# Moving two pre-pass steps across a pair boundary, and sharing a subtraction between GpSimd and VectorE, in a four-layer attention kernel

## The chip, the cores and the metric

The kernel runs on one core of a Trainium2 chip. The metric is the device time of one execution in microseconds (us). The kernel before took 4373.35 us in the median of three runs (4364.13 to 4380.87); less is better.

A core has engines that each work through their own queue in order: TensorE for matrix products (PE in the profile, with its weight loads as PEld), VectorE (DVE), ScalarE (ACT), GpSimd (POOL), and SyncE (SP), whose queue here issues most of the transfers. They wait for one another through semaphores. Matrix products are written to PSUM, from where VectorE and ScalarE read them; everything else lies in SBUF.

## The reference

The input is `x` of shape (4, 32, 32, 384) in float32, four images of 1024 positions with 384 channels. Four layers follow, each with a normalisation before and a residual sum after it. Two of them matter here.

Layer 0 is attention with six heads of 64 channels. The keys and values come from positions that are sampled with learned offsets, and a bias is sampled bilinearly from a table:

```python
attn = jnp.einsum('bmhc,bnhc->bhmn', qh, k) * scale
...
attn = jax.nn.softmax(attn + bias, axis=-1)
out = jnp.einsum('bhmn,bnhc->bmhc', attn, v).reshape(Bq, Hq, Wq, NC)
```

Layer 1 is attention with twelve heads of 32 channels. Its softmax is multiplied by a weight that comes from a second, coarse similarity, and is then divided by column sums:

```python
sim = jax.nn.sigmoid(sim_beta + sim_alpha * jnp.einsum('bhnd,bhmd->bhnm', _l2norm(xg_h), _l2norm(gc)))
group_weight = jnp.einsum('bhnm,bhkm->bhnk', sim, sim)
gamma = jax.nn.sigmoid(group_gamma)
group_weight = group_weight * gamma + (1.0 - gamma)
attn = jax.nn.softmax(jnp.einsum('bhnd,bhmd->bhnm', q, k) * scale, axis=-1)
attn = attn * group_weight
attn = attn / (attn.sum(axis=2, keepdims=True) + 1e-08)
out = jnp.einsum('bhnm,bhmd->bhnd', attn, v)
```

Layer 2 takes ratios of box sums, layer 3 is a local attention over 3 x 3 neighbourhoods. The change doesn't touch them.

## The kernel before

**Two lanes.** The work of an image is split into a front lane (layer 0) and a trunk lane (layers 1 to 3). Layer 0 of image 0 runs first by itself, in another form (`heads0`). From then on `Net.layer3` steps through the trunk of image b and, by the weights that the generators yield, lets the front lane of image b+1 run in between. So while images 0, 1 and 2 are in their trunk, the heads of the next image's layer 0 are mixed into the same queues; image 3's trunk has nothing beside it. Within the order in which the program names the instructions, a scheduler places them on the engines by priority, by the buffers that come free, and by `issue_after`, which holds a block of instructions behind a named one.

**The front lane's heads** (`Front.head0`). A head is done in two halves of 512 queries; 12 halves an image, 36 in all for images 1 to 3. For each of eight blocks of 128 keys (`j`), GpSimd gathers a window of the bias table (L944), ScalarE and VectorE interpolate it in two directions (L956, L957, L961, L962), two matmuls (L968) give the scores, and VectorE adds them to the bias (L971) and keeps a running maximum `rmax` (L973, L975). After the eighth block the maximum over keys is wanted for every query, in every partition: `rmax` is transposed on PE (L982), VectorE takes the maximum `top` (L986), GpSimd multiplies it by the identity matrix (L988, `diag`, 128 x 512), PE multiplies that by ones (L990), and ScalarE copies the result to `tb` (L994). Then, for each block, VectorE subtracts `tb` from the scores (L1001), ScalarE takes exponentials (L1002), and PE multiplies them with the values (L1003).

**The trunk lane's pairs** (`Trunk.pair`). Layer 1 takes its twelve heads in six pairs, p = 0 to 5. The keys are in eight blocks of 128, j = 0 to 7. For each block and each half of the queries, PE computes scores for the two heads (L1699) into one of the two tiles called `big`, and ScalarE takes their exponential (L1707). The logarithm of the softmax's denominators has been put into an extra row of the queries, so that these exponentials are the softmax already. GpSimd scales the similarity block `sg` (L1682). Then `product(h, r)` runs four times: PE forms the group weights by transposing what an earlier block has kept (L1724) and by multiplying `sg` with `sim` (L1729), VectorE multiplies them onto the softmax with a running sum (L1736), and ScalarE keeps what later blocks need (L1741). `values` scales the values by the column sums (L1662, L1663, L1665) and multiplies (L1671), one block behind.

**The pre-pass.** The denominators of pair p+1 are computed while pair p runs. That takes eight steps, `sums_step(i)`, one for each block of 128 queries. A step takes both `big` tiles: four matmuls (L1561), then for each tile a maximum on VectorE (L1570) and an exponential with a sum on ScalarE (L1574), both at high priority. Only after that is the tile free for the next scores. The results collect in `nmax` and `den` (one buffer each). In the kernel before the eight steps of pair p are placed so: two at j = 0, two at j = 1, one each at j = 2 to 5, either between the second and third product or after the fourth. At the end of j = 5, `sums_log` turns the sums into logarithms (L1592 to L1598), and `load_sums(p + 2)` reloads the pre-pass's own copies `q4` and `k4` by four SP transfers (L1522, L1523). At j = 6, `sums_row` transposes the result (L1605, L1607) and `load_lse` puts it into the next pair's queries. Also at j = 6, after that, `sims(0)`, and at j = 7 `sims(1)`, compute the next pair's coarse similarity: four matmuls each into both `big` tiles (L1618), a tanh on ScalarE (L1627) and an addition on VectorE (L1630).

The last pair (p = 5) has no pre-pass. Pair 0's successor is prepared in pair 0 itself, and the first pair's own before the loop.

Of the kernel before, what the change touches and what calls it, by code (L numbers as in the profile page):

```python
# [21 lines left out]
ALU = mybir.AluOpType  # L22
# [4 lines left out]
P = 128  # L27
# [5 lines left out]
NH1, HD1 = 12, 32  # L33
# [33 lines left out]
def bc(ap, axis, n):  # L67

    u = ap.unsqueeze(axis)
    shape = list(u.shape)  # L70
    shape[axis] = n
    return u.broadcast_to(shape)
# [357 lines left out]
class Front(Lane):  # L430
# [500 lines left out]
    def head0(self, h, q):  # L931

        nc, v = self.nc, self.nc.vector
        f = self.f
        k, r0 = h // 2, (h % 2) * GC
        rows = slice(r0, r0 + GC)
        HH, HN = HW // 2, N // 2
        queries = self.qpad[rows, k, 1 + HH * q : 1 + HH * (q + 1), 1 : 1 + HW]
        logits = []
        rmax = self.wt([P, HN], "rmax", 2)  # L940
        for j in range(NJ):
            c = j * G + h
            win = self.wt([P, (HH + 1) * WROW], "win", 4)
            nc.gpsimd.indirect_dma_start(  # L944
                out=win,
                out_offset=None,
                in_=self.strips[:, :],
                in_offset=bass.IndirectOffsetOnAxis(
                    ap=self.widx[:, q, c : c + 1], axis=0
                ),  # L950
            )
            wv = win.rearrange("p (r c) -> p r c", c=WROW)
            sc = lambda i, t: f[:, i, t, c : c + 1]

            z = self.wt([P, HH, HW + 1], "z", 3)
            nc.scalar.activation(z, wv[:, 0:HH, 0 : HW + 1], AF.Copy, scale=sc(1, 1))  # L956
            v.scalar_tensor_tensor(  # L957
                z, wv[:, 1 : HH + 1, 0 : HW + 1], sc(0, 1), z, ALU.mult, ALU.add
            )
            lg = self.wt([P, HH, HW], "lg", 13)  # L960
            nc.scalar.activation(lg, z[:, :, 0:HW], AF.Copy, scale=sc(1, 0))  # L961
            v.scalar_tensor_tensor(lg, z[:, :, 1 : HW + 1], sc(0, 0), lg, ALU.mult, ALU.add)  # L962
            logits.append(lg.rearrange("p y x -> p (y x)"))
            if j % 2:
                ps = [self.bank() for _ in range(2)]
                for u in range(2):
                    w, mov = self.logits_of(h, q, j - 1 + u)
                    nc.tensor.matmul(ps[u], w, mov, start=True, stop=True)  # L968
                for u in range(2):
                    lf = logits[j - 1 + u]  # L970
                    v.tensor_tensor(lf, ps[u], lf, ALU.add)  # L971
                    if j - 1 + u == 1:
                        v.tensor_tensor(rmax, logits[0], lf, ALU.max)  # L973
                    elif j > 1:
                        v.tensor_tensor(rmax, rmax, lf, ALU.max)  # L975
                yield 6


        NI = HN // P
        ps = self.bank()  # L980
        for i in range(NI):
            nc.tensor.transpose(  # L982
                ps[:, i * P : (i + 1) * P], rmax[:, i * P : (i + 1) * P], self.ident
            )
        top = self.wt([P, NI], "top", 2)
        v.tensor_reduce(top, ps.rearrange("p (i n) -> p i n", i=NI), AX.X, ALU.max)  # L986
        diag = self.wt([P, NI, P], "diag", 1)
        nc.gpsimd.tensor_tensor(diag, bc(self.ident, 1, NI), bc(top, 2, P), ALU.mult)  # L988
        ps = self.bank()
        nc.tensor.matmul(  # L990
            ps, self.ones, diag.rearrange("p i n -> p (i n)"), start=True, stop=True
        )
        tb = self.wt([P, HN], "tb", 2)
        nc.scalar.copy(tb, ps)  # L994
        yield 3


        po = self.bank()
        for j in range(NJ):
            lf = logits[j]  # L1000
            v.tensor_tensor(lf, lf, tb, ALU.subtract)  # L1001
            nc.scalar.activation(lf, lf, AF.Exp)  # L1002
            nc.tensor.matmul(po, self.values_of(h, j), lf, start=j == 0, stop=j == NJ - 1)  # L1003
            if j % 2:
                yield 2

        nc.scalar.copy(queries, po[rows, :].rearrange("p (y x) -> p y x", y=HH))
        den = self.sums_of(h, po, logits[0])
        nc.sync.dma_start(self.den[h][:, q * HN : (q + 1) * HN], den)
        yield 3  # L1010
# [303 lines left out]
class Trunk(Lane):  # L1314
# [317 lines left out]
    def pair(self, p):  # L1632
# [1 line left out]


        nc, v = self.nc, self.nc.vector
        st = self.sums_state() if p + 1 < NH1 // 2 else None
        qa, ka = self.qks[p % 2]
        sim = self.sim
        if p == 5:  # L1640
# [38 lines left out]
        for j in range(NJ):  # L1679
# [66 lines left out]
            for h, r in parts[:split]:  # L1746
                last = product(h, r)
            with self.tc.issue_after(last):
                if st and j < 2:
                    self.sums_step(2 * j, st)  # L1750
                elif st and j < 6:
                    self.sums_step(j + 2, st)
                elif st and j == 6:
                    self.sums_row(p + 1, logs)
                    self.load_lse(p + 1)
                    self.sims(0)
            yield 7
            for h, r in parts[split:]:
                last = product(h, r)
            with self.tc.issue_after(last):  # L1760
                if st and j < 2:
                    self.sums_step(2 * j + 1, st)
                elif st and j == 7:
                    self.sims(1)
            if late:
# [1 line left out]
            late.append((j, es, tot))  # L1767
            if st and j == 5:
                logs = self.sums_log(st)
                if p + 2 < NH1 // 2:  # L1770
                    self.load_sums(p + 2)
            yield 7
        values(*late.pop())
        y = self.wt([P, 512], "y")
# [378 lines left out]
```

## Time and profile before

| what | value |
|---|---|
| median of three runs | 4373.35 us (4364.13 to 4380.87) |
| profiled execution | 4344.14 us, of which span 4342.2 us |
| mean granted clock of TensorE | 0.949 |
| busy: PE / VectorE / ScalarE / GpSimd | 90% / 72% / 53% / 22% of the span |
| chain that ended last: PE / VectorE / ScalarE | 49% / 27% / 9% of the span |
| a pair of layer 1, images 0 to 2 | about 119 to 126 us |
| a pair of layer 1, image 3 | about 77 us |

The profile is one execution, and it was 29 us shorter than the median. In a row of groups of instructions stand the line of the kernel, the engine, the operation, what it writes and reads by the program's names, the shape and the number of instructions; after the first bar their busy time in us and the mean duration of one in ns; after the second the idle time of that engine just before them, and what ended most of it. In a row of the timeline stand the start and the duration in us, then the same, and in brackets the idle time before. In a row of windows stand the stretch, its length, the busy time of PE, PEld, VectorE, ScalarE and GpSimd with the number of instructions, the granted clock of TensorE, the share of the DMA engines and the GB/s. Lines are those of the kernel before; in the kernel after, those behind L1001 are higher by one and, from L1753 on, by up to nine.

### The profile page before, as it was taken

What the parts mean: (1) busy time and instruction counts of PE and PEld (TensorE: products, weight loads), DVE (VectorE), ACT (ScalarE), POOL (GpSimd) and SP (SyncE); (2) the same over time, 40 slices, a digit from 0 to 9 for tenths busy, and PEclk for the clock granted to TensorE, in tenths of its full rate; (3) what the DMA queues carried; (4) which work ended last, traced back from release to release, by engine and by line L of the source; (5) the groups of instructions that cost most, each with busy time, mean ns of one, the idle gap of its engine ahead of it and who ended that gap; (6) DMA issues with size and microseconds to landing.
All of it is one profiled execution on the core that took longest, in us unless ns stands there. A gap on an engine that the chain in (4) does not pass through costs nothing.

```text
span 4342.2 us, 45288 instructions
## 1 busy us (share of the span) xinstructions
PE 3921.3 (90%) x14832; PEld 1681.8 (39%) x14832; DVE 3109.8 (72%) x5905; ACT 2304.8 (53%) x3638; POOL 963.9 (22%) x979
## 2 busy tenths in 40 slices
PE   8788989998999898999899989889889999999998
PEld 4333434333334443433333444333333434444444
DVE  4799676878887456787878746578887874566654
ACT  3366344666664334566766423366676642566633
POOL 1754152212121105221212101431121301000000
PEclk9999989998999998999999999899999999999999
DMA  7744353212221455321212154432221214311111
GB/s 161 236 122 118 89 157 106 64 42 81 60 81 40 127 140 147 108 65 46 75 54 81 40 159 143 132 103 60 61 75 47 75 41 134 99 43 26 33 34 44
DMA packets 295397, 385.08 MB, mean 89 GB/s; under 512 B 167858, under 2 KB 228798, under 8 KB 294650
## 3 DMA queue, kind: packets, MB, share of 16 engines
q1 hardware_dynamic: 246336, 217.44, 17.7%
q0 software_dynamic: 39936, 145.53, 11.3%
q10 hardware_dynamic: 8890, 19.23, 1.3%
q8 instruction: 118, 1.93, 0.2%
q14 instruction: 117, 0.96, 0.1%
HBM read 295.63 MB, written 86.75 MB: 88 GB/s over the span
## 4 chain that ended last, share of the span: by engine, by line
PE 49%; DVE 27%; ACT 9%; issue 8%; DMA 4%; POOL 3%; SPq 0%; DVEq 0%; ACTq 0%; POOLq 0%
PE bank L1729 10%; PE big L1699 6%; DVE nmax L1570 4%; PE big L407 4%; PE bank L1003 4%; DVE e L1736 3%; PE bank L421 3%; PE big L1561 3%; ACT big L1574 3%; PE bank L1724 2%; PE bank L1671 2%; PE big L667 2%; DVE z L1122 2%; PE bank L968 2%; DMA win<-strips,widx 2%
## 5 line engine op out<-in xcount | busy, mean ns | idle before, releaser
L1729 PE MATMUL bank<-whole,sg 128*128 128x512 f32 (+3 forms) x2304 | 854.4, 501 | 7.7 <-POOL sg L1682 6.2
L1736 DVE SCALAR_TENSOR_TENSOR e<-bank,gam,e 128x512 f32<-128x512 f32 x768 | 560.4, 747 | 309.9 <-PE bank L1729 189.2
L1574 ACT ACTIVATE big<-big,nmax 128x1024 f32<-128x1024 f32 x384 | 417.5, 1087 | 295.9 <-DVE nmax L1570 294.1
L1729 PEld LDWEIGHTS bank<-whole,sg 128*128 128x128 f32 x2304 | 401.7, 197 | 357.8 <-issue 272.1
L1699 PE MATMUL big<-qa,ka 64*128 64x512 f32 x1536 | 451.6, 669 | 86.7 <-ACT big L1574 82.5
L1570 DVE TENSOR_REDUCE nmax<-big 128x1 f32<-128x1024 f32 x384 | 451.9, 1217 | 62.8 <-PE big L1561 62.8
L1707 ACT ACTIVATE e<-big 128x1024 f32<-128x1024 f32 x384 | 382.1, 1020 | 176.3 <-PE big L1699 166.8
L944 POOL DMA_INDIRECT win<-strips,widx x288 | 314.8, 1093 | 699.8 <-DVE z L957 382.2
L1682 POOL TENSOR_SCALAR sg<-whole,gam 128x512 f32<-128x512 f32 x192 | 149.1, 777 | 1348.1 <-PE bank L1729 1073.0
L1561 PE MATMUL big<-k,q 32*128 32x512 f32 x1536 | 270.2, 670 | 41.6 <-ACT big L1574 30.5
L1699 PEld LDWEIGHTS big<-qa,ka 64*128 64x128 f32 x1536 | 146.9, 197 | 345.1 <-ACT big L1574 177.9
L1003 PE MATMUL bank<-lg,va 128*128 128x512 f32 x576 | 268.2, 607 | 12.9 <-ACT lg L1002 12.9
L751 POOL DMA_INDIRECT gat<-pairs,sidx x192 | 214.6, 1118 | 290.5 <-DVE ix_one L550 233.2
L962 DVE SCALAR_TENSOR_TENSOR lg<-z,bias_f,lg 128x512 f32<-128x512 f32 x288 | 216.3, 768 | 48.9 <-ACT lg L961 47.3
L956 ACT ACTIVATE z<-win,bias_f 128x528 f32<-128x528 f32 x288 | 205.3, 736 | 57.2 <-DVE lg L962 26.2
L1001 DVE TENSOR_TENSOR lg<-lg,tb 128x512 f32<-128x512 f32 x288 | 182.0, 689 | 74.7 <-ACT tb L994 74.7
L957 DVE SCALAR_TENSOR_TENSOR z<-win,bias_f,z 128x528 f32<-128x528 f32 x288 | 214.9, 763 | 20.9 <-ACT z L956 19.0
L1671 PE MATMUL bank<-e,vs 128*32 128x512 f32 x1536 | 210.7, 617 | 17.7 <-DVE vs L1665 17.7
L1741 ACT COPY gn<-bank 128x128 f32<-128x128 f32 (+2 forms) x288 | 106.3, 370 | 209.6 <-DVE e L1736 208.7
L961 ACT ACTIVATE lg<-z,bias_f 128x512 f32<-128x512 f32 x288 | 199.9, 716 | 16.8 <-DVE z L957 13.2
L971 DVE TENSOR_TENSOR lg<-bank,lg 128x512 f32<-128x512 f32 x288 | 191.3, 683 | 12.7 <-PE bank L968 12.0
L968 PE MATMUL bank<-qs,kz 64*128 64x512 f32 x288 | 172.5, 683 | 12.2 <-DVE e L1736 8.5
(326 smaller groups left out, 6315.1 us busy)
## 6 DMA issues: line engine op xcount, KB each, us to landing
q<-qd SPq DMA_DIRECT2D x48, 256.0 KB
xg<-xgd SPq DMA_DIRECT2D x48, 256.0 KB
pairs<-gat SPq DMA_DIRECT2D x48, 192.0 KB
w<-in_gmat SPq DMA_DIRECT2D x15, 576.0 KB
w<-in_Wqkv SPq DMA_DIRECT2D x12, 576.0 KB
a<-in_x SPq DMA_DIRECT2D x16, 384.0 KB
q<-qpad SPq DMA_DIRECT2D x12, 512.0 KB
qs<-q SPq DMA_DIRECT2D x24, 256.0 KB
```

Source lines behind the costliest of these rows:

```text
L944: nc.gpsimd.indirect_dma_start(out=win, out_offset=None, in_=self.strips[:, :], in_offset=bass.IndirectOffsetOnAxis(ap=self.widx[:, q, c : ...
L962: v.scalar_tensor_tensor(lg, z[:, :, 1 : HW + 1], sc(0, 0), lg, ALU.mult, ALU.add)
L968: nc.tensor.matmul(ps[u], w, mov, start=True, stop=True)
L1003: nc.tensor.matmul(po, self.values_of(h, j), lf, start=j == 0, stop=j == NJ - 1)
L1561: nc.tensor.matmul(ps[r][:, h * 512 : (h + 1) * 512], self.q4[rows, i * P : (i + 1) * P], self.k4[rows, 0:512], start=True, stop=True,)
L1570: top = v.tensor_reduce(nmax[:, r, i : i + 1], ps[r], AX.X, ALU.max, negate=True)
L1574: nc.scalar.activation(ps[r], ps[r], AF.Exp, bias=nmax[:, r, i : i + 1], accum_out=den[:, r, i : i + 1],)
L1671: nc.tensor.matmul(av[r0 : r0 + HD1, :], vs[:, r, :], es[h][:, r, :], start=j == 0, stop=j == NJ - 1,)
L1699: nc.tensor.matmul(ps[:, r, :], ka[rows, j * P : (j + 1) * P], qa[rows, cols], start=True, stop=True,)
L1707: nc.scalar.activation(e, ps, AF.Exp)
L1729: last = nc.tensor.matmul(ps[:, (mid - i0) * P :], sg[:, r, m, :], sim[:, h, r, m, (mid - i0) * P :], start=m == 0, stop=m == 1,)
L1736: v.scalar_tensor_tensor(e[:, r, :], ps, self.gam[:, 1:2], e[:, r, :], ALU.add, ALU.mult, accum_out=tot[:, r, h : h + 1],)
```

## The change

There are two edits that have nothing to do with each other.

In `Front.head0`, the diagonal is made by VectorE rather than GpSimd, and the subtraction of the maxima goes to GpSimd for every second block (j odd). Over 36 halves that takes 36 instructions from GpSimd and gives it 144, and the reverse on VectorE. `heads0`, the form for image 0, stays.

In `Trunk.pair`, steps 0 and 1 of a pre-pass move to the end of the pair before: step 0 to the middle of j = 6, after `sums_row`, and step 1 to the middle of j = 7. `sims(0)` goes from the middle of j = 6 to its end. The buffers `nmax` and `den` for it are taken at j = 6, after `sums_log` has read the old ones, and are handed on in `self.st`. `load_sums(p + 2)`, which the moved steps need, goes from the end of j = 5 to its middle, right after step 7. Pair 0 keeps two steps at j = 0 and at j = 1, since nothing ran before it. So pairs 1 to 4 have one step in each of j = 0 to 5, and pairs 0 to 3 one more at j = 6 and at j = 7. That moves 8 steps an image, 32 in all.

```diff
-        nc.gpsimd.tensor_tensor(diag, bc(self.ident, 1, NI), bc(top, 2, P), ALU.mult)
+        v.tensor_tensor(diag, bc(self.ident, 1, NI), bc(top, 2, P), ALU.mult)
...
         for j in range(NJ):
             lf = logits[j]
-            v.tensor_tensor(lf, lf, tb, ALU.subtract)
+            eng = nc.gpsimd if j % 2 else v
+            eng.tensor_tensor(lf, lf, tb, ALU.subtract)
             nc.scalar.activation(lf, lf, AF.Exp)
...
-        st = self.sums_state() if p + 1 < NH1 // 2 else None
+        st, self.st = (self.st if p else self.sums_state()), None
...
             with self.tc.issue_after(last):
-                if st and j < 2:
+                if st and p == 0 and j < 2:
                     self.sums_step(2 * j, st)
                 elif st and j < 6:
                     self.sums_step(j + 2, st)
+                    if j == 5 and p + 2 < NH1 // 2:
+                        self.load_sums(p + 2)
                 elif st and j == 6:
                     self.sums_row(p + 1, logs)
                     self.load_lse(p + 1)
-                    self.sims(0)
+                    if p + 2 < NH1 // 2:
+                        self.st = self.sums_state()
+                        self.sums_step(0, self.st)
+                    else:
+                        self.sims(0)
+                elif self.st:
+                    self.sums_step(1, self.st)
             yield 7
...
             with self.tc.issue_after(last):
-                if st and j < 2:
+                if st and p == 0 and j < 2:
                     self.sums_step(2 * j + 1, st)
+                elif st and j == 6 and self.st:
+                    self.sims(0)
                 elif st and j == 7:
                     self.sims(1)
...
             if st and j == 5:
                 logs = self.sums_log(st)
-                if p + 2 < NH1 // 2:
-                    self.load_sums(p + 2)
             yield 7
```

## The prediction

> **What bounds the kernel now.** I read the page's busy times first, then its costliest groups, then the idle time of TensorE (PE) slot by slot through all 24 pairs of heads, then windows of the places that the change touches, then single steps in the timeline.
>
> ```profile
> PE 3921.3 (90%) x14832; PEld 1681.8 (39%) x14832; DVE 3109.8 (72%) x5905; ACT 2304.8 (53%) x3638; POOL 963.9 (22%) x979
> ...
> L1574 ACT ACTIVATE big<-big,nmax 128x1024 f32<-128x1024 f32 x384 | 417.5, 1087 | 295.9 <-DVE nmax L1570 294.1
> ...
> L1699 PE MATMUL big<-qa,ka 64*128 64x512 f32 x1536 | 451.6, 669 | 86.7 <-ACT big L1574 82.5
> L1570 DVE TENSOR_REDUCE nmax<-big 128x1 f32<-128x1024 f32 x384 | 451.9, 1217 | 62.8 <-PE big L1561 62.8
> ...
> L1001 DVE TENSOR_TENSOR lg<-lg,tb 128x512 f32<-128x512 f32 x288 | 182.0, 689 | 74.7 <-ACT tb L994 74.7
> ```
>
> PE is busy 90% of the span, so only about 421 us are idle, and the largest single cause of that idle time is one edge: the scores L1699 waiting 82.5 us for L1574, the exponentials of a pre-pass step. A step fills both "big" tiles, VectorE (DVE) takes two maxima, ScalarE (ACT) two exponentials, and only then may another matmul write there. In the timeline, one step of image 3 and, last, the scores after the worst wait and after none:
>
> ```profile
> 3961.74 1.14 PE L1561 MATMUL big<-k,q 32*128 32x512 f32 x8
> 3962.98 2.36 DVE L1570 TENSOR_REDUCE nmax<-big 128x1 f32<-128x1024 f32 x2 [0.31 <-PE big L1561]
> 3964.30 1.09 ACT L1574 ACTIVATE big<-big,nmax 128x1024 f32<-128x1024 f32 x1 [1.22 <-DVE nmax L1570]
> 3965.43 1.09 ACT L1574 ACTIVATE big<-big,nmax 128x1024 f32<-128x1024 f32 x1
> 3965.55 0.30 PEld L1699 LDWEIGHTS big<-qa,ka 64*128 64x128 f32 x4 [1.04 <-ACT big L1574]
> 3966.68 0.30 PEld L1699 LDWEIGHTS big<-qa,ka 64*128 64x128 f32 x4 [0.83 <-ACT big L1574]
> ```
>
> ```profile
> 1032.11 3.78 PE L1699 MATMUL big<-qa,ka 64*128 64x512 f32 x8 [5.10 <-ACT big L1574]
> ```
>
> ```profile
> 4050.03 1.99 PE L1699 MATMUL big<-qa,ka 64*128 64x512 f32 x8
> ```
>
> From a step's first matmul the first tile is free after 3.8 us (3961.74 to 3965.55), the second after 4.95 (3966.68). And the eight score matmuls after a 5.10 us gap took 3.78 us instead of 1.99: PE restarted at half rate, worth 1.8 us more. I see the same after gaps of 3.25, 2.44, 1.91 and 1.27 us, and not after 0.9 to 1.2.
>
> The last view is the windows. The first two rows are the end of pair 2 (j=6, 7) and the start of pair 3 (j=0, 1) in image 0, the last two the same places in image 3, where no layer-0 lane runs beside.
>
> ```profile
> 975.00:1006.30 31.30, 24.13 (x103) 11.35 (x107) 29.20 (x64) 17.63 (x27) 9.01 (x9) 0.80 0.31 88
> 1006.30:1053.90 47.60, 39.25 (x126) 14.46 (x120) 43.02 (x72) 39.10 (x65) 18.93 (x18) 0.89 0.40 117
> ```
>
> ```profile
> 4044.60:4058.70 14.10, 14.10 (x97) 7.60 (x99) 10.11 (x29) 9.66 (x13) 1.39 (x2) 1.00 0.25 70
> 4058.70:4085.00 26.30, 25.52 (x98) 9.74 (x94) 16.32 (x31) 17.08 (x29) 1.39 (x2) 1.00 0.11 28
> ```
>
> The columns are length, then busy time of PE, PEld, DVE, ACT, POOL. In image 0 DVE is busy 93 and 90% in the two places; in image 3 PE is busy 100% at j=6, 7 and idle only 0.78 us at j=0, 1. So the change moves work from where PE waits to where either DVE (images 0 to 2) or PE (image 3) is already full.
>
> **Moved steps, gain.** Per image, four of the five doubled starts lose a step at j=0 and one at j=1; pair 0 keeps its own. PE's idle time before L1699 there, j=0 plus j=1, is in image 0: pair 1 3.38+0.82, pair 2 1.19+0.99, pair 3 5.10+3.25, pair 4 2.44+0.99, together 18.2 us. Slots j=2 and j=3, with one step each, have 0.00, so I expect nearly all of it gone. Four of these gaps are long enough for a half-rate restart, at about 1.7 us each: 6.8. Upper bound 25 us per image, 75 for images 0 to 2. Image 3 gains 4 x 0.78 = 3.
>
> **Moved steps, cost.** At j=6 and j=7 a step now stands before the two sims groups (L1618), which need the same two big tiles. Image 3 before: L1618 at 4046.73, followed by products to 4049.03, L1671 (1.0 us for four), and L1699 at 4050.03, no gap. After, the step takes that place (T): products until T+2.3, one L1671 until about T+2.8, but the first tile is free only at T+3.8 (1.0 idle), the second at T+4.95 while its half of L1618 is ready at T+4.3 (0.6). At j=7 the products are shorter (T+2.0) but four L1671 stand between (T+3.0): 0.8 plus 0.6. That is 3.0 us per transition, less the 0.78: +2.2, times 4 = +9 us. The half-rate restart (1.8) stays away if gaps stay near 1.0.
>
> In images 0 to 2 two L968 matmuls cover some of j=7, so the PE bound is 2.1 us per transition. The other bound is DVE: two steps are four maxima, 4 x 1.13 = 4.5 us more in a place where it has little idle time, with e (L1736) and vs (L1665) queued behind them and PE behind those; call it 4.9. I take 3.5, the middle, since only pair 2's end is at 93% DVE and the others are at 78 to 86%. By transition: into pair 1, 4.2+1.7-3.5 = 2.4 gained; into pair 2, 2.2-3.5 = -1.3; into pair 4, 3.4+1.7-3.5 = 1.6; into pair 3 the PE account gives 8, but the two windows leave DVE only 6.7 us idle in 78.9, and it cannot all go, so 3. Sum 5.7 an image, 17 for three. Net of image 3: **-8 us**.
>
> The reload of q4/k4 (four SP DMAs per pair) is issued half a slot earlier, as its reader now comes earlier. In image 3 the old issue ran 4039.69 to 4042.07 with its traffic over near 4045, and the first new reader stands behind 4046.5; some 2 us of slack, 7 in the other images. Cost nothing; uncovered it would be up to 2 us at 16 places. On SP the four L1281 transfers now stand behind it, nobody waits for them at once.
>
> **The diagonal on DVE.** PE's L990 waits for it:
>
> ```profile
> L990 PE MATMUL bank<-diag,ones x72: 592/697/1063, 760.3 to 3547.9; 128*128 128x512 f32 x72
> ...
>   POOL diag L988: 75.4, 63
> ```
>
> Of these 75.4 us (with weight loads) PE itself idles 23.4, in 27 of the 36 halves. POOL takes 1.04 us for it; the nearest DVE row of the same size is L1001 at 0.69, and one crossing between engines goes. I take 0.45 us saved in 27 halves: **-12 us** (between -5 and -18; nothing queued on DVE in front of it, L1001 waits for it anyway through tb).
>
> **Half the subtractions on POOL.** 36 halves, four each. If POOL and DVE ran freely side by side, DVE would be relieved of 4 x 0.6 - 0.6 (diag) = 1.8 us per half. The trace says they don't run freely: a DVE operation with two SBUF inputs beside a POOL computation.
>
> ```profile
> 1024.46 1.14 DVE L957 SCALAR_TENSOR_TENSOR z<-win,bias_f,z 128x528 f32<-128x528 f32 x1 [0.26 <-ACT z L956]
> ...
> 1024.97 1.19 POOL L1682 TENSOR_SCALAR sg<-whole,gam 128x512 f32<-128x512 f32 x1
> ...
> 1025.52 1.18 DVE L962 SCALAR_TENSOR_TENSOR lg<-z,bias_f,lg 128x512 f32<-128x512 f32 x1
> ```
>
> All three take 0.69 to 0.76 undisturbed, so here they took turns. L1001 itself has two such inputs. If each POOL subtraction (1.04, the diagonal's size) excludes DVE's, eight take 4 x 0.6 + 4 x 1.04 = 6.6 us against 4.8: 1.8 us later per half, +65 us if all of it were on the path. But L1736, L1570 and L971, which read PSUM, show no such stretch, and they fill much of DVE's row in these slots; and ACT, which takes 0.62 per exponential besides L1707, finished the eight some 7.5 us after tb before. Behind the POOL block stand the gathers (L944) and sg (L1682); POOL is 22% busy, and L1729 waited only 6.2 us for sg in all. PE's idle time behind DVE (L1671, L968, L1724, L982, L1605) is about 62 us in all; a tenth of it relieved is **-6 us**, range -25 to +40.
>
> The Trainium skill, "SBUF — State Buffer", section "Who interferes with whom", speaks against this edit: the pair of ports that the two engines share is an exclusive lock for a whole instruction when DVE has two SBUF inputs and GpSimd reads SBUF. By the rule taken alone the term would be the +65 bound, and by the PSUM rows the -6. On the restart, "TensorE: Matmul & The Clock Gate", section "What's actually happening", wants an idle window of some 3.4 us; by it only the 5.10 gap would count surely, and the clock term would be 1.8 instead of 6.8 an image; the trace shows it after 1.27.
>
> **Sum.** -8 -12 -6 = -26 us. The profiled execution took 4344.14 us (span 4342.2 and 1.94 around it), 29 under the median of 4373.35; the terms scale by 0.7%, so the forecast is 4347 as a median (own range 4330 to 4366).
>
> **Rivals.**
> *Everything regained (faster):* the 75 us go, costs stay at 2.1 a transition (-50), image 3 +9, diagonal -12, DVE relieved by -10: -63, 4310. For it: the 0.00 at j=2, 3. Against it: DVE at 91%.
> *The wait only moves (slower):* the gap before L1618 passes 1.27 us, restarts PE at half rate, and DVE's four maxima are paid in full: 4.9+1.8 against 4.6 regained, +2.1 at 12 places; image 3 4 x (3.0+1.8-0.8) = +16; diagonal -12: +29, 4402. It decides once a transition costs over 6.3 at its end. For it: 93% DVE; against: most ends at 78%.
> *Turns on the shared inputs (slower):* about 0.6 of the 65 us reach the path, because e7 and the odd exponentials come late and hold L1707 behind them on ACT: -8 -12 +40 = +20, 4393. It decides above 1.1 us a half.
> That the change doesn't do what it says is excluded: in the built order each moved instruction is where the diff puts it, and the totals move by 36 and 144.
>
> **Chances.** Forecast 0.48, all regained 0.22, moved wait 0.16, turns 0.14. About 0.5% (22 us) is what a measurement can tell: half of the forecast's case and the first rival are beyond it (0.46), most of the two slower ones (0.26), the rest within (0.28). The range runs from past the fast rival to just past the slow one, 4300 to 4405.
>
> **What would show it.** Right: L1699's wait for L1574 falls from 82.5 to near 30 (pair 0's share, some 22, stays), L1618 gains a wait for L1574 of 40 to 60 us, L990's wait falls by a third, image 3's pairs grow from 76.7 to about 79 us. Wrong: L1618's wait above 80 or L1671's and L968's waits for DVE grown (wait moved); L1001 above 0.9 us mean and L1003's wait for L1002 above 40 (turns); pairs of images 0 to 2 shorter by 4 us each (all regained).

## The result: slower by 0.65%

The kernel after took 4395.68 us in the median of six runs (4388.47 to 4403.08), the kernel before 4365.74 us in the median of six as well (4360.40 to 4380.87). The ratio is 1.0065, with an interval of 1.0051 to 1.0080: about 28 us more (30 by the medians), where 26 us less had been forecast.

The page and the groups of the kernel after, with the lines that answer to those of before (L1002 is the subtraction, L1571 and L1575 the pre-pass's maximum and exponential, L1700 the scores, L1619 the sims, L1004 the values' matmul):

```profile
PE 3974.2 (90%) x14832; PEld 1692.1 (39%) x14832; DVE 3159.8 (72%) x5797; ACT 2303.2 (52%) x3638; POOL 1171.6 (27%) x1087
...
L1575 ACT ACTIVATE big<-big,nmax 128x1024 f32<-128x1024 f32 x384 | 417.7, 1088 | 327.6 <-DVE nmax L1571 289.9
...
L1571 DVE TENSOR_REDUCE nmax<-big 128x1 f32<-128x1024 f32 x384 | 452.8, 1218 | 82.9 <-PE big L1562 61.4
...
L1700 PE MATMUL big<-qa,ka 64*128 64x512 f32 x1536 | 416.0, 637 | 32.4 <-ACT big L1575 24.3
...
L1004 PE MATMUL bank<-lg,va 128*128 128x512 f32 x576 | 275.5, 619 | 34.2 <-ACT lg L1003 34.2
...
L1002 POOL TENSOR_TENSOR lg<-lg,tb 128x512 f32<-128x512 f32 x144 | 238.3, 1685 | 189.6 <-ACT tb L994 189.6
...
L1002 DVE TENSOR_TENSOR lg<-lg,tb 128x512 f32<-128x512 f32 x144 | 206.4, 1481 | 53.7 <-ACT tb L994 53.7
```

Two readings stand against each other. The wait that the moved steps were to remove did go: L1700 waits 24.3 us for L1575, against 82.5. But VectorE's subtraction takes 1481 ns instead of 689, so 144 of them cost 206 us where 288 cost 182 before: VectorE has half the subtractions and spends 24 us more on them. (Its whole busy time rose by 50 us with 108 instructions fewer; the other half of that is the diagonal, 24.8 us.) GpSimd's take 1685 ns. And PE's wait for the exponentials, L1004 here, grew from the 12.9 us that it had as L1003 in the kernel before to 34.2 us:

```profile
L1003 PE MATMUL bank<-lg,va 128*128 128x512 f32 x576 | 268.2, 607 | 12.9 <-ACT lg L1002 12.9
```

The timeline of one half, in pair 3 of image 0, shows what happens. Three subtractions of VectorE and four of GpSimd are released by the same copy `tb`:

```profile
1102.65 0.59 ACT L994 COPY tb<-bank 128x512 f32<-128x512 f32 x1 [0.65 <-PE bank L990]
1103.27 4.05 DVE L1002 TENSOR_TENSOR lg<-lg,tb 128x512 f32<-128x512 f32 x3 [1.90 <-ACT tb L994]
1103.32 6.37 POOL L1002 TENSOR_TENSOR lg<-lg,tb 128x512 f32<-128x512 f32 x4 [4.04 <-ACT tb L994]
```

The two engines start 0.05 us apart. VectorE's first, which began first, takes 0.69 us; from then on each waits out the other's instruction, and VectorE needs 4.05 us for three. In the kernel before the same three took 1.90:

```profile
1079.30 1.90 DVE L1001 TENSOR_TENSOR lg<-lg,tb 128x512 f32<-128x512 f32 x3 [2.96 <-ACT tb L994]
```

None of the 144 subtractions of VectorE ran without one of GpSimd beside it. Of the 144, 30 took 0.69 us, the first of its half each time, and 114 were longer.

The windows of the two transitions that the prediction showed, now in the kernel after; first image 0 (end of pair 2, start of pair 3), then image 3 (end of pair 3, start of pair 4):

```profile
1001.60:1036.10 34.50, 26.77 (x119) 10.80 (x121) 34.50 (x65) 23.62 (x35) 9.95 (x8) 0.90 0.30 84
1036.10:1078.90 42.80, 37.00 (x111) 13.71 (x109) 37.74 (x59) 34.48 (x58) 22.98 (x19) 0.92 0.37 106
```

```profile
4094.40:4115.30 20.90, 19.72 (x113) 8.80 (x114) 14.65 (x33) 14.28 (x21) 1.39 (x2) 1.00 0.19 52
4115.30:4136.10 20.80, 20.80 (x76) 8.02 (x74) 11.70 (x26) 12.28 (x20) 1.39 (x2) 1.00 0.12 30
```

In image 0 the end grew by 3.2 us and the start shrank by 4.8; VectorE is now busy 100% at the end. In image 3 the end grew by 6.8 us (14.1 to 20.9) and the start shrank by 5.5. By these two places the steps are not a loss of 28 us; the first experiment decides it.

One caution on profiled executions. The kernel before's was 4344.14 us and the kernel after's 4395.69, a difference of 52 us where the medians differ by 30. Of these 52, 24.5 lie before the first exponential of layer 1's pairs in image 0 (L1707), in code that the change does not touch: it came at 627.7 us in one and at 652.2 us in the other. Four kernels measured next, on a chip where before took 4370 us, had it at 651 to 657 us, whatever their edit; the eight after them, on chips where before took 4332 to 4338, had it at 629 to 639. In what follows the medians and ratios decide on totals; the traces are compared by single instructions and by stretches of layer 1.

### The profile page after: what moved, and what is told of

Its sections match the earlier page's. It is cut to its first block, busy times and chain, and to the rows that moved or that the text cites. A ratio compares the mean times of both kernels' runs of the same rounds, so it can differ in the third digit from the quotient of the medians.

```text
span 4393.9 us, 45304 instructions
## 1 busy us (share of the span) xinstructions
PE 3974.2 (90%) x14832; PEld 1692.1 (39%) x14832; DVE 3159.8 (72%) x5797; ACT 2303.2 (52%) x3638; POOL 1171.6 (27%) x1087
## 4 chain that ended last, share of the span: by engine, by line
PE 51%; DVE 25%; issue 9%; ACT 8%; DMA 4%; POOL 3%; SPq 1%; another core or an unknown queue 0%; ACTq 0%; DVEq 0%; POOLq 0%
PE bank L1730 11%; PE big L1700 5%; PE big L1562 4%; PE big L407 4%; DVE nmax L1571 4%; PE bank L1004 3%; PE bank L421 3%; DVE e L1737 3%; ACT big L1575 2%; PE bank L1725 2%; PE bank L1672 2%; PE bank L968 2%; DVE lg L962 2%; PE big L1879 2%; DVE z L1123 2%
## 5 line engine op out<-in xcount | busy, mean ns | idle before, releaser
L1737 DVE SCALAR_TENSOR_TENSOR e<-bank,gam,e 128x512 f32<-128x512 f32 x768 | 559.9, 746 | 286.8 <-PE bank L1730 183.9
L1575 ACT ACTIVATE big<-big,nmax 128x1024 f32<-128x1024 f32 x384 | 417.7, 1088 | 327.6 <-DVE nmax L1571 289.9
L1571 DVE TENSOR_REDUCE nmax<-big 128x1 f32<-128x1024 f32 x384 | 452.8, 1218 | 82.9 <-PE big L1562 61.4
L1700 PE MATMUL big<-qa,ka 64*128 64x512 f32 x1536 | 416.0, 637 | 32.4 <-ACT big L1575 24.3
L1562 PE MATMUL big<-k,q 32*128 32x512 f32 x1536 | 286.9, 665 | 64.8 <-issue 26.7
L1004 PE MATMUL bank<-lg,va 128*128 128x512 f32 x576 | 275.5, 619 | 34.2 <-ACT lg L1003 34.2
L1002 POOL TENSOR_TENSOR lg<-lg,tb 128x512 f32<-128x512 f32 x144 | 238.3, 1685 | 189.6 <-ACT tb L994 189.6
L962 DVE SCALAR_TENSOR_TENSOR lg<-z,bias_f,lg 128x512 f32<-128x512 f32 x288 | 216.7, 769 | 56.1 <-ACT lg L961 54.4
L1700 PEld LDWEIGHTS big<-qa,ka 64*128 64x128 f32 x1536 | 144.2, 192 | 274.0 <-issue 120.6
L1002 DVE TENSOR_TENSOR lg<-lg,tb 128x512 f32<-128x512 f32 x144 | 206.4, 1481 | 53.7 <-ACT tb L994 53.7
L1672 PE MATMUL bank<-e,vs 128*32 128x512 f32 x1536 | 231.2, 632 | 12.1 <-DVE vs L1666 10.7
L956 ACT ACTIVATE z<-win,bias_f 128x528 f32<-128x528 f32 x288 | 205.8, 736 | 49.2 <-DVE lg L962 24.8
L957 DVE SCALAR_TENSOR_TENSOR z<-win,bias_f,z 128x528 f32<-128x528 f32 x288 | 217.9, 772 | 15.9 <-ACT z L956 11.0
L1003 ACT ACTIVATE lg<-lg 128x512 f32<-128x512 f32 x288 | 164.9, 623 | 74.8 <-POOL lg L1002 60.8
```

The lines of the kernel that those rows point to most:

```text
L1002: eng.tensor_tensor(lf, lf, tb, ALU.subtract)
L1562: nc.tensor.matmul(ps[r][:, h * 512 : (h + 1) * 512], self.q4[rows, i * P : (i + 1) * P], self.k4[rows, 0:512], start=True, stop=True,)
L1571: top = v.tensor_reduce(nmax[:, r, i : i + 1], ps[r], AX.X, ALU.max, negate=True)
L1575: nc.scalar.activation(ps[r], ps[r], AF.Exp, bias=nmax[:, r, i : i + 1], accum_out=den[:, r, i : i + 1],)
L1672: nc.tensor.matmul(av[r0 : r0 + HD1, :], vs[:, r, :], es[h][:, r, :], start=j == 0, stop=j == NJ - 1,)
L1700: nc.tensor.matmul(ps[:, r, :], ka[rows, j * P : (j + 1) * P], qa[rows, cols], start=True, stop=True,)
```

## The experiments

Theory A: GpSimd's and VectorE's subtractions take turns, and that is the loss. Theory B, the rival: the moved steps only move the wait. Theory C: the loss lies in the unchanged stretches. The first four kernels take the change apart.

**Moved steps alone.** The edit is against the kernel after:

```diff
-        v.tensor_tensor(diag, bc(self.ident, 1, NI), bc(top, 2, P), ALU.mult)
+        nc.gpsimd.tensor_tensor(diag, bc(self.ident, 1, NI), bc(top, 2, P), ALU.mult)
...
-            eng = nc.gpsimd if j % 2 else v
-            eng.tensor_tensor(lf, lf, tb, ALU.subtract)
+            v.tensor_tensor(lf, lf, tb, ALU.subtract)
```

> Only the two pre-pass steps are moved; diagonal on GpSimd and all eight subtractions on VectorE as in the kernel before. Theory A (GpSimd's subtractions take turns with VectorE's and that is the loss): about the time of before, ratio 0.996 to 1.002, with the scores' wait for the pre-pass exponentials near 25 us instead of 82 and the sims' wait near 28. Theory B (the moved steps only move the wait and cost image 3 and VectorE more): slower, ratio 1.004 to 1.008. Theory C (the loss is stalls in parts whose code is unchanged, layer 0 of image 0 and the intake of layer 1): profile shows layer 1 of image 0 starting near 650 us instead of 628 in this kernel too.

Measured: ratio 0.9963 (0.9948 to 0.9979), 15 us faster by the medians. B falls; the ratio is at the lower edge of what A expected. The waits went where the prediction put them:

```profile
L1699 PE MATMUL big<-qa,ka 64*128 64x512 f32 x1536 | 424.2, 638 | 32.6 <-ACT big L1574 26.9 <-ACT whole L1627 2.8 <-ACT e L1707 1.4
...
L1618 PE MATMUL big<-xg,gc 32*128 32x512 f32 x384 | 112.0, 724 | 31.7 <-ACT big L1574 28.4 <-ACT whole L1627 3.0
```

In the kernel before the sims had

```profile
L1618 PE MATMUL big<-xg,gc 32*128 32x512 f32 x384 | 70.2, 701 | 3.0 <-ACT whole L1627 3.0
```

The scores lost 55.6 us of waiting, the sims gained 28.4. The sims' matmuls are also busy 112 us instead of 70, and the scores' 424 instead of 452, which no reading of idle time alone would show. C falls here: the pairs of image 0 start at 653 us, yet the kernel is faster than before on the same chip.

**The diagonal and the subtractions, without the steps.** The two hunks of `head0` on the kernel before.

> Only the diagonal on VectorE and the odd subtractions on GpSimd; the pre-pass steps stay. Theory A: slower, ratio 1.004 to 1.009, subtractions near 1.5 us on VectorE and 1.7 us on GpSimd, values' wait for the exponentials 30 us or more. Theory B: ratio 0.996 to 1.001. Theory C: start of layer 1 of image 0 near 650 us.

Measured: 1.0070 (1.0045 to 1.0095), 32 us slower, subtractions of 1516 ns on VectorE and 1648 ns on GpSimd, L1004's wait for the exponentials 35.6 us. As A expected.

**The diagonal alone.**

```diff
-        nc.gpsimd.tensor_tensor(diag, bc(self.ident, 1, NI), bc(top, 2, P), ALU.mult)
+        v.tensor_tensor(diag, bc(self.ident, 1, NI), bc(top, 2, P), ALU.mult)
```

> Only the diagonal on VectorE, all eight subtractions on VectorE. Theories A and B: 8 to 14 us faster than before, ratio 0.997 to 0.998, the wait of the ones-matmul for the diagonal down from 24 to about 9 us. Theory C: start of layer 1 of image 0 near 650 us and no faster than before.

Measured: 0.9927 (0.9905 to 0.9949), 29 us faster by the medians, more than twice what was expected. The ones-matmul's wait for the diagonal fell as expected, from the first of these rows (before) to the second:

```profile
L990 PE MATMUL bank<-diag,ones 128*128 128x512 f32 x72 | 43.0, 680 | 24.1 <-POOL diag L988 23.9
```

```profile
L990 PE MATMUL bank<-diag,ones 128*128 128x512 f32 x72 | 40.0, 638 | 14.9 <-DVE diag L988 14.9
```

Against this kernel the previous one, which differs only in putting the odd subtractions on GpSimd, is slower by 4401.72 - 4341.10 = 61 us. That is 1.7 us per half, nearly the 1.8 that the prediction gave as its upper bound.

**Steps and diagonal, no subtraction on GpSimd.**

> Moved steps and the diagonal on VectorE, all subtractions on VectorE: the kernel after without its GpSimd subtractions. Theory A: faster than before by 10 to 20 us, ratio 0.995 to 0.998. Theory B: slower, ratio 1.002 to 1.006. Theory C: like the kernel after, 1.004 to 1.008, with late starts of layer 1.

Measured: 0.9910 (0.9886 to 0.9933), 37 us faster, better than even A expected. The kernel after is this one with half the subtractions on GpSimd, and 1.0065 / 0.9910 = 1.0156 is some 68 us. Beside the moved steps the edit costs about as much as without them.

What makes the two engines exclude each other is tested next. **VectorE's subtraction reads the maxima from PSUM.** The edit is against the kernel after:

```diff
             eng = nc.gpsimd if j % 2 else v
-            eng.tensor_tensor(lf, lf, tb, ALU.subtract)
+            eng.tensor_tensor(lf, lf, tb if j % 2 else ps, ALU.subtract)
```

> The kernel after, but VectorE's four subtractions read the maxima from the PSUM bank that the ones-matmul wrote, not from their copy tb in SBUF, so that they have one SBUF input; GpSimd's four still read tb. Theory A1 (the two engines exclude each other because both subtractions need a shared way into SBUF): VectorE's subtraction falls from 1.48 to about 0.69 us, GpSimd's from 1.68 to 1.05 to 1.2 us, and the time falls by 35 to 60 us against the kernel after, ratio to before 0.990 to 0.999. Theory A2 (GpSimd's queue, with the gathers and sg behind the block, or its slower exponentials, are the loss): VectorE's subtraction shrinks, but the ratio stays at 1.003 to 1.007. Theory A3 (any two engines reading SBUF share its speed): durations stay above 1.3 us.

Measured: 0.9932 (0.9915 to 0.9948). One operand fetched from elsewhere turns the kernel after from 0.65% slower to 0.7% faster than before, a change of 1.3% or 58 us, as A1 expected. The same half as above:

```profile
1076.24 1.88 DVE L1002 TENSOR_TENSOR lg<-lg,bank 128x512 f32<-128x512 f32 x3 [1.90 <-ACT tb L994]
1076.29 5.00 POOL L1002 TENSOR_TENSOR lg<-lg,tb 128x512 f32<-128x512 f32 x4 [4.04 <-ACT tb L994]
```

The start is the same, 0.05 us apart, but VectorE's three take 1.88 us again. Over the whole run:

```profile
L1002 DVE TENSOR_TENSOR lg<-lg,bank x144: 632/680/689, 773.8 to 3503.7; 128x512 f32<-128x512 f32 x144
L1002 POOL TENSOR_TENSOR lg<-lg,tb x144: 1253/1279/1757, 773.9 to 3506.6; 128x512 f32<-128x512 f32 x144
```

Here stand minimum, median and maximum in ns. In the kernel after they were

```profile
L1002 DVE TENSOR_TENSOR lg<-lg,tb x144: 691/1753/1769, 792.4 to 3594.8; 128x512 f32<-128x512 f32 x144
L1002 POOL TENSOR_TENSOR lg<-lg,tb x144: 1268/1722/1777, 792.4 to 3596.0; 128x512 f32<-128x512 f32 x144
```

so A1 holds: it is the second SBUF input of VectorE's instruction. A3 (any two engines) falls, and so does A2 (GpSimd's queue) as an account of the whole loss. The edit also ends the common reading of one tile, `tb`; that a common tile isn't needed is in the prediction's rows, where L957 and L962 took turns with L1682 and shared none with it. GpSimd's subtraction takes 1.28 us and not the 1.05 to 1.2 expected; the diagonal, from which the 1.04 came, had repeating inputs, and whether that is the reason was not tested.

The variant is not faster than steps and diagonal without any split (0.9932 against 0.9910, intervals that overlap). ScalarE waits 39.4 us in it for GpSimd's subtractions, and PE 27.6 us for the exponentials, against 16.1 without the split. So the collision explains the loss, but even without it the sharing gained nothing that shows.

**All eight subtractions on GpSimd** (steps moved, diagonal on VectorE, `nc.gpsimd.tensor_tensor(lf, lf, tb, ALU.subtract)` for every j).

> Moved steps, diagonal on VectorE, and all eight subtractions on GpSimd, none on VectorE. Theory A1: without VectorE's subtractions beside, GpSimd's take 1.05 to 1.2 us save where they meet other VectorE operations with two SBUF inputs; the eight then last about 8.5 to 10 us, a little longer than the 6.9 of the kernel after, while VectorE is free: ratio 1.000 to 1.012. Theory A2: clearly slower than the kernel after, 1.012 or more.

Measured: 1.0206 (1.0188 to 1.0225), beyond both expectations of A1, in the range of A2.

```profile
L1001 POOL TENSOR_TENSOR lg<-lg,tb 128x512 f32<-128x512 f32 x288 | 366.0, 1312 | 184.0 <-ACT tb L994 184.0
...
L1002 ACT ACTIVATE lg<-lg 128x512 f32<-128x512 f32 x288 | 180.5, 629 | 156.5 <-POOL lg L1001 156.5
```

At 1312 ns apiece the eight take 10.5 us, not 8.5 to 10, and ScalarE waited 156.5 us for them. So GpSimd's slowness is a loss of its own once it holds the whole row; in the PSUM variant, where GpSimd has four, ScalarE's wait for it is the 39.4 us.

One number goes with these ratios in the main: the time from the end of `top` (L986) to the end of the eighth exponential, from the trace, mean of 36 halves.

| kernel | us from top to the eighth exponential | ratio to before |
|---|---|---|
| before (two profiles) | 11.0, 10.8 | 1 |
| diagonal alone | 10.4 | 0.9927 |
| diagonal and half the subtractions on GpSimd | 11.8 | 1.0070 |
| steps and diagonal | 10.7 | 0.9910 |
| after | 11.8 | 1.0065 |
| after, VectorE reading PSUM | 10.0 | 0.9932 |
| all eight on GpSimd | 14.0 | 1.0206 |

From steps and diagonal to after it is 1.15 us, times 36 = 41, beside 68 us of run time, and from the diagonal alone to the kernel with subtractions 1.4, times 36 = 50, beside 61 us. This is not a full account: the PSUM variant has the shortest chain and not the best ratio, and a kernel further down (the diagonal on ScalarE) has a longer chain than after, 12.8, and no larger a loss. The rest is not traced; VectorE's own longer row, with L1737 behind it, is a candidate that was only argued.

**Three kernels toward a better one.** First, all eight subtractions on VectorE and from PSUM, without the copy (the edit is shown against steps and diagonal):

```diff
-        tb = self.wt([P, HN], "tb", 2)
-        nc.scalar.copy(tb, ps)
...
-            v.tensor_tensor(lf, lf, tb, ALU.subtract)
+            v.tensor_tensor(lf, lf, ps, ALU.subtract)
```

> Moved steps, diagonal on VectorE, all eight subtractions on VectorE and all reading the maxima from PSUM; ScalarE's copy to tb is left out. If what the diagonal's move gained was the length of the chain from maximum to first subtraction (and the TensorE clock behind it), another 0.6 to 0.7 us off that chain gains again: ratio 0.984 to 0.990 against before, 0.991 being the same kernel with the copy. If the chain is hidden by now, 0.991; if the bank held during eight subtractions makes matmuls wait for a bank, 0.993 to 1.000.

Measured: 0.9899 (0.9882 to 0.9915), against 0.9910 with the copy: inside each other's intervals, so no gain is shown. The chain to the first exponential is 1.0 us shorter (3.4 us after top instead of 4.4), to the eighth only 0.4; most of the gain is lost again on the way through the eight.

Second, the steps moved only while a front lane runs beside:

```diff
+        self.moved = b < NB - 1
...
+        two = p == 0 or not self.moved
...
-                if st and p == 0 and j < 2:
+                if st and two and j < 2:
```

> Moved steps only in images 0 to 2, the last image's pairs as in the kernel before; diagonal on VectorE, all subtractions on VectorE. The profile of the moved steps showed image 3's layer 1 longer by 10 us (440.8 to 451.0) and images 0 to 2 shorter. If that is the steps' whole cost, this is 10 us faster than moved steps plus diagonal: ratio 0.987 to 0.990, image 3's layer 1 at 441 us.

Measured: 0.9889 (0.9872 to 0.9905); layer 1 of image 3 is 440.4 us long, from 451.0. The 10 us are there in the trace; the ratio's step from 0.9910 is within the intervals.

Third, both:

> Moved steps in images 0 to 2 only, diagonal on VectorE, all subtractions on VectorE and reading the maxima from PSUM, no copy to tb. The two last steps each gave 5 to 9 us by themselves: together 0.985 to 0.989 against before. If they overlap, 0.989 to 0.990.

Measured: 0.9856 (0.9835 to 0.9877), 4273.77 us against 4338.28 on the same chip, faster than before and after. It is below each of its parts as well (0.9899 and 0.9889), though its interval just touches that of the second.

**Why did the diagonal gain more than twice what was expected?** Three more kernels. A filler matmul on TensorE in the kernel before:

```diff
         ps = self.bank()
+        nc.tensor.matmul(ps, self.ones, rmax, start=True, stop=True)
         nc.tensor.matmul(
             ps, self.ones, diag.rearrange("p i n -> p (i n)"), start=True, stop=True
```

> The kernel before (diagonal on GpSimd, all subtractions on VectorE, steps unmoved) with one matmul more per half, ones times rmax, whose result is overwritten: it fills TensorE's idle time between the transposes and the ones-matmul without making the chain shorter. It adds 36 matmuls of about 0.9 us (33 us of work) and can cover about 23 us of idle time. Theory K (the diagonal's move gained 28 us rather than 12 because the gap before the ones-matmul no longer drops TensorE to half rate): the time lost to the lower granted clock falls by about 18 us in images 0 and 1 of the trunk as it did with the diagonal on VectorE, and the ratio is 0.994 to 0.999. Theory L (it gained because the chain is shorter): the clock's loss stays, and the ratio is 1.001 to 1.005.

Measured: 1.0039 (1.0025 to 1.0054). By its ratio, Theory L; but the time lost to the lower clock (the sum of all stretches at half clock, halved) was 204 us, against 221 us in the first profile of before, which would be K, and 192 us in the second, further down. The filler ran straight after the transposes, and PE still waited 13.4 us for the diagonal, up to 1.47 us at a time. It separates nothing by itself.

**The diagonal on ScalarE,** as four scaled copies:

```diff
-        nc.gpsimd.tensor_tensor(diag, bc(self.ident, 1, NI), bc(top, 2, P), ALU.mult)
+        for i in range(NI):
+            nc.scalar.activation(
+                diag[:, i, :], self.ident, AF.Copy, scale=top[:, i : i + 1]
+            )
```

> The kernel before with the diagonal made by ScalarE, as four copies of the identity scaled by a column of top each, about 0.27 us apiece: 1.0 to 1.2 us in all, as long as GpSimd's 1.04, but GpSimd's queue is free of it, so the gathers behind don't wait for the maximum. If the diagonal's move to VectorE gained by freeing GpSimd's queue, this gains as well: ratio 0.993 to 0.996. If it gained by the shorter chain (0.35 us and what TensorE's clock adds), this gains nothing: ratio 0.999 to 1.004.

Measured: 1.0058 (1.0038 to 1.0077), slower than either expectation. A copy took 389 ns and not 270, so the diagonal took 1.6 us, and the chain to the eighth exponential 12.8 us. That is 1.8 to 2.0 us more than before, 65 to 71 us over 36 halves, and the run is longer by 25 us only, so the length of this chain is no price by itself. The longer chain may also hide a gain of the freed queue, so the ratio doesn't separate the two. A wait does: ScalarE's for the gathered windows (L956 for `win`), which the diagonal in GpSimd's queue could delay, is 19.6 and 20.1 us in the two profiles of before, 17.6 us here and 17.0 us with the diagonal on VectorE. A free queue took 2 to 3 us off it, little beside 29.

**The kernel before once more.**

> The kernel before once more, for a second profile of it: how far the time lost to the lower granted clock and the lengths of the unchanged stretches differ from one execution to the next. If the clock's loss of 36, 37 and 27 us in the layer-1 stretches of images 0, 1 and 2 belongs to the kernel, it is within 3 us of that again; if it is chance, it moves by 10 us or more as it did between images with the diagonal on VectorE (19, 19, 31).

Measured: 0.9998 (0.9983 to 1.0013). The clock's loss in layer 1 of images 0, 1 and 2 was 23, 21 and 23 us where the first profile had 36, 37 and 27; over the whole run 192 against 221 us. Two of the three moved by more than 10 us, the third by 4: by the stated test it is mostly chance, and a single profile can't show that the diagonal's gain is one of clock. The second profile does allow a comparison at nearly equal clock. From the first to the last exponential (L1707) of layer 1, images 0 to 2 took 2123.0 us together in it and 2103.3 us with the diagonal alone, with 67 and 69 us lost to the clock. These stretches hold 30 of the 36 halves, and 20 us of shortening there need no Theory K. It is one profile each, on two chips.

## Why the prediction was wrong

**The step that failed** is the term for the subtractions on GpSimd, taken as -6 us with a range of -25 to +40. It measured +61 us without the moved steps and about +68 with them. The prediction had the mechanism (instructions of the kernel before that took turns, 1.14 to 1.19 us each), it had a price for it (+65, if all of it were on the path), and it had the page of the Trainium skill that names it, "SBUF — State Buffer", section "Who interferes with whom"; the runs agree with that page: the exclusion goes when VectorE's second input is not in SBUF. It then put that price at nothing, because VectorE's operations that read PSUM fill much of its row, and counted a gain instead, a tenth of PE's waits behind VectorE. Neither held. What decides here whether the two streams meet is what releases them: both halves of the subtractions wait for the same `tb`, and in 30 of 36 halves they start 0.05 us apart, so what else VectorE does in the slot has little say. And the waits behind VectorE did not ease: in the five lines that the prediction names, PE's grew from about 59 to 65 us when the subtractions joined the diagonal, and from 49 to 56 us when they joined steps and diagonal.

The rival "turns on the shared inputs" was right in mechanism and in sign. That its 4393 us lies 3 us from the measured median is luck: its +40 was 21 to 28 us too small, and the -20 for steps and diagonal beside it too small by about as much. The +65 came close by luck in part as well. It used the diagonal's 1.04 us for GpSimd; with the 1.28 us measured there and 0.69 us on VectorE the same working gives 2.4 us a half, 85 us in all, of which 61 to 68 came through.

**The moved steps** were right in sign, and -15 us against a forecast of -8. L1700 waits 24.3 us (near 30 said), and layer 1 of image 3 grew by 10.2 us (440.8 to 451.0, from the first to the last exponential) against +9. The working for one transition, +2.2 us, is 79.0 - 76.8 in pairs 2 and 3. Its place was off: in the window of image 3 above PE idles 1.2 us, where 3.0 us of idle time had been counted, and the sims' longer busy time was not foreseen; L1619's wait is 28.4 us, below the 40 to 60 said.

**The diagonal** was right in sign and too small: -12 forecast (-18 at most), -29 measured. PE's wait in L990 behaved as forecast, 9 us less with the diagonal alone (23.9 to 14.9); beside the moved steps, which had already brought it to 15.9, it fell by 6.7 to 9.2. The chain to the eighth exponential got shorter by 0.4 to 0.6 us in the mean of all 36 halves, 16 to 22 us, where 27 halves had been counted, and layer 1 by 20 us at nearly equal clock. What is left of the 29 is open.

**The clock term** of the steps, 1.7 us after each of four gaps an image, can't be confirmed: two profiles of the same kernel differ by 29 us in the clock's loss. The length of a gap does not decide either, which the prediction's reading passed over. In the profile of before, the first of these two gaps (2.53 us) was followed by full clock, a granted 1.00 from 643.6 to 646.0, the second, a little shorter (2.44 us), by a mean of 0.56 from 1153.6 to 1157.1:

```profile
643.67 2.26 PE L1699 MATMUL big<-qa,ka 64*128 64x512 f32 x8 [2.53 <-ACT big L1574]
```

```profile
1153.64 3.43 PE L1699 MATMUL big<-qa,ka 64*128 64x512 f32 x8 [2.44 <-ACT big L1574]
```

The pieces measured apart add up to less than the whole: the moved steps (0.9963) and the two edits of `head0` (1.0070) make 1.0033, against 1.0065. The difference is about what the intervals allow, and an interaction of the two is neither shown nor excluded.

## What to carry to other kernels

When work is split over two engines, look first at what releases the two parts: if it is one event, they meet every time, as in these 36 halves, and the price of full exclusion belongs in the middle of the range, not at its end. Where VectorE and GpSimd must run together, feed one of VectorE's two inputs from PSUM; here that one operand was worth 1.3% of the run. But ask first whether the split is wanted: VectorE alone was as fast as the split without collisions. A change of several edits should be forecast, and measured, one by one: here the steps gained 15 us, the diagonal 29, and the subtractions lost 61 to 68.

## What the runs showed of the hardware

A float32 subtraction of 128 x 512 takes 0.68 to 0.69 us on VectorE and 1.28 us on GpSimd. Side by side with both inputs in SBUF they take 1.75 and 1.72 us in the median, not much under the 1.97 us that both need one after the other; with one input of VectorE's in PSUM, 0.68 and 1.28. It does not always go turn by turn: three times in the kernel with the diagonal and the subtractions alone, one subtraction of VectorE lasted 5.53 us, through all four of GpSimd's.

The granted clock of TensorE drops to 0.50 in stretches of 3.41 us and multiples of it, 79 of them in the first profile of before and 66 in the second. Half of that time is 221 and 192 us in two executions of one and the same kernel; it is the most that the lower clock can have cost, since PE is not busy throughout. The spread of 29 us is as large as what the diagonal's edit moved.
